# A post-norm transformer layer on one core: Q and K two batches ahead, their parts written once and filled from broadcasts

## The chip, the cores and the metric

One Trainium2 chip; the kernel runs on 1 core. Times are device microseconds (us) of one execution; lower is better. The kernel before has a median of 2144.75 us in 3 runs (2143.95 to 2145.74).

## What is computed

Eight sequences ("batches") of 1024 rows and 256 columns go through one layer, all in float32. Cut to what matters:

```
scores = (Q @ K.T) / sqrt(16) + prior_lambda * mask(|i - j|)     # 16 heads of 16
attn   = softmax(scores);  a = (attn @ V) @ Wo.T + bo
x      = layernorm(x + a)
h      = x @ (tern(w_fc) * s).T + gate * (x @ v.T @ fast_b.T @ u.T)
y      = (relu(h) ** 2) @ (tern(w_proj) * s).T
out    = layernorm(x + y)
```

The weights w_fc and w_proj are rounded to -1, 0, 1 times a scale per row; the mask is a sum of two Gaussian bells around the diagonal.

## The kernel before

**The groups.** The loop of L1508 runs over 512 groups, 64 per batch and 16 for each set of 4 heads (called G below; 32 G in all). One group handles two blocks of 128 keys of a pair of heads: TensorE makes scores e with keys on the partitions (L761, 2 tiles of 128 x 1024; near the diagonal the prior is added by TensorE, L742, or by VectorE, L775), ScalarE takes the exponential (L776), and TensorE weighs V with the exponentials of the group before (L791). The softmax needs the row maxima first: 12 groups ahead (`LEAD`), TensorE makes the same scores with queries on the partitions (s, L665) and VectorE takes the maximum of each row (L677, 2 per group). All e and s tiles come from a ring of three PSUM tiles. Every 8 groups (group 5 of each 8) `set_max` (L688 to L711) turns the maxima into rows: TensorE transposes them (L693), ScalarE and GpSimd split them (L699, L700), SP writes them to DRAM (L702) and four DMAs put them into the stacks of Q (L709).

Twelve groups before the first e (group -12 on), only s and maxima run: the lead-in.

**Stacks.** A stack holds for one head 64 rows of split Q or K (16 dimensions, each as a high and a low part, in the four combinations) and two rows for the maxima. There are two slots of stacks, each for one G: 2 pairs of heads (pr) x 2 heads (a) x K and Q, that is 8 tiles. `fill_stack` (L321, DMA at L315 to L318) reloads a slot at the start of the G before: 8 DMAs of 256 KB, issued by SP, each from 64 rows of 4 KB. The first pair of stacks is read 4 groups later, the second 8 groups later.

**Where the stacks come from.** A Q/K piece (L611) is four matmuls for 128 columns of heads over 256 rows of x; after two pieces ScalarE casts the result to its high part (`two`, L630, one buffer), GpSimd subtracts for the low part (L631), and `write_parts` (L199 to L206) writes it to DRAM: K as two DMAs of 512 KB, Q as one of 512 and two of 256 KB, since the DRAM tile has four planes per row.

**Pieces.** In each group TensorE also does a few pieces of other work from a list of jobs: Q/K pieces (L611), V (L584), transposes of x (L558), the output projection (L991), the feed-forward of the batch before (L1024, 1038, 1065, 1100), and in the first batch the preparation of the ternary weights (L432 to L550; its low-rank part waits for GpSimd at L494). They share one PSUM bank of two halves. A budget per group ("filled") decides how many pieces it takes. Batch b makes the second chunk (128 columns) of Q and K of its own, and the first chunk of those of b + 1.

**Normalizing.** When a chunk of heads is done, deferred steps follow: the sums are read back as `den` (L829), one group later VectorE takes the reciprocal (L834), `back` goes to DRAM (L836), `rec` is read as a broadcast over 16 rows (L841) with the raw output (L844), and GpSimd multiplies (L848). In the last batch one half is done apart (L878 to L887, `rec_third`). The residual's x is loaded (L976) and gets a bias on GpSimd (L982).

**Order.** The program fixes the order of the instructions on every engine as they are written (L1632 on), so SP issues its DMAs, and ScalarE does its work, in the order of the code. DMAs take eight semaphores in turn, and DMA n is issued only when DMA n - 8 has landed.

The lines on which the change turns:

```python
two = p1.tile([P, 2, HALF], F32R, tag="two", name=f"two{name}_{b}_{c}_{half}")   # L629, p1 has bufs=1
nc.scalar.copy(two[:, 0, :], full)                                               # L630
...
queue.dma_start(                                                                 # L316
    stack[name, s, pr, a][at : at + P // 2, cols].bitcast(F32),
    parts_of[name, b, g // 2][src : src + HD, :, cols].rearrange("p l n -> (p l) n"),
)
```

Of the kernel before, what the change touches and what calls it, by code (L numbers as in the profile page):

```python
# [10 lines left out]
F32 = mybir.dt.float32  # L11
# [32 lines left out]
def tile_postln_layer(  # L44
# [44 lines left out]
    dpool = ctx.enter_context(tc.tile_pool(name="dpool", bufs=2, space=bass.MemoryType.DRAM))  # L89
    first = len(nc.cur_bb.bb.instructions)  # L90
# [11 lines left out]
    def load_x(b, half, tag="x"):  # L102
        t = p1.tile([P, QB, D], F32, tag=tag, name=f"x_{b}_{half}")
        nc.sync.dma_start(t, x[b, ts(half, HALF), :].rearrange("(t p) d -> p t d", p=P))
        x_of[b, half] = t

    load_x(0, 0)
# [85 lines left out]
    def new_parts(name, b, c):  # L193
        parts_of[name, b, c] = dpool.tile(
            [P, 4, L], F32, tag=f"parts_{name}", name=f"parts_{name}_{b}_{c}"
        )
        return parts_of[name, b, c]

    def write_parts(name, t, two, half, rows=slice(0, P)):  # L199
        to, two = t[rows, :, ts(half, HALF)], two[rows].bitcast(F32)  # L200
        nc.sync.dma_start(to[:, :2], two)
        if name == "k":
            nc.sync.dma_start(to[:, 2:], two)
        else:
            nc.sync.dma_start(to[:, 2, :], two[:, 1, :])
            nc.sync.dma_start(to[:, 3, :], two[:, 0, :])  # L206
# [106 lines left out]
    def fill_one(name, G, pr, a, queue, cols=slice(0, L)):  # L313
        (b, g), s = divmod(G, NG), G % SLOTS
        at, src = P // 2 * a, HD * ((g % 2) * HG + 2 * pr + a)  # L315
        queue.dma_start(  # L316
            stack[name, s, pr, a][at : at + P // 2, cols].bitcast(F32),
            parts_of[name, b, g // 2][src : src + HD, :, cols].rearrange("p l n -> (p l) n"),  # L318
        )
# [60 lines left out]
    now, jobs = -LEAD, []  # L380
# [50 lines left out]

    def prepare_fc(half):  # L432
# [4 lines left out]
        def first():  # L437
            w = p1.tile([P, n, D], F32, tag="hi", name=f"fc_{half}")
            nc.sync.dma_start(w, w_fc[ts(half, n * P), :].rearrange("(c p) d -> p c d", p=P))
            st["w"] = w  # L440
            st["uT"] = p1.tile([R, HALF], F32, tag="x1T", name=f"uT_{half}")
            pus = [misc(f"pu_{half}_{k}") for k in range(2)]
            for k, pu in enumerate(pus):
                for i in range(2):
                    nc.tensor.matmul(
                        pu[:R, ts(i, P)],
                        u_sb[:, n * half + 2 * k + i, :],
                        ident,
                        start=True,
                        stop=True,  # L450
                    )

            def empty():
                for k, pu in enumerate(pus):
                    nc.scalar.copy(st["uT"][:, ts(k, D)], pu[:R, :])

            return empty
# [9 lines left out]
        def tern(i, pf):  # L467
            w, hc = st["w"][:, i, :], n * half + i
            sc = s_fc[:, hc : hc + 1]
            scales(sc, w, D)  # L470
            ternary(w, sc, f"fc_{half}_{i}")
            full = p1.tile([P, R], F32, tag="lowf", name=f"lowf_{half}_{i}")
            nc.scalar.copy(full, pf)

            def rows():

                inv = p2.tile([P, 1], F32, tag="inv", name=f"inv_{half}_{i}")
                nc.vector.reciprocal(inv, sc)
                nc.gpsimd.tensor_scalar(full, full, inv, gate_c, op0=ALU.mult, op1=ALU.mult)
                low = ones_low[:, 1, :].rearrange("p (a b c r) -> p a b c r", a=2, b=2, c=2)  # L480
                for k in range(2):
                    src = full.unsqueeze(1).to_broadcast([P, 2, R])
                    nc.gpsimd.tensor_copy(low[:, k, 0].bitcast(F32R), src)
                    nc.gpsimd.tensor_sub(low[:, k, 1], src, low[:, k, 0])
                st["rows"] = i

            defer(1, rows)

        def piece(i):
# [20 lines left out]
            (0.5, lambda i=i: piece(i), 2, lambda i=i: st.get("rows") == i) for i in range(n)  # L510
        ]

    def prepare_proj(i):
# [4 lines left out]
        def first():  # L518
            st["w"] = p1.tile([P, FF], F32, tag="hi", name=f"proj_{i}")
            nc.sync.dma_start(st["w"], w_proj[ts(i, P), :])  # L520

        def second():
            st["sc"] = p2.tile([P, 1], F32, tag="sc", name=f"sc_proj_{i}")
            scales(st["sc"], st["w"], FF)
            st["diag"] = p1.tile([P, D], F32, tag="x1T", name=f"diag_{i}")[:, :P]
            nc.gpsimd.tensor_scalar_mul(st["diag"], ident, st["sc"])
            ternary(st["w"][:, :D], st["sc"], f"proj_{i}_0")
# [20 lines left out]
        return [(0.01, first, 0), (0.01, second, 0), (0.3, third, 1)] + [  # L548
# [4 lines left out]
    def transpose_x(b, bank):  # L553
        def piece(half, dc, k):
# [9 lines left out]
            if dc == NDC - 1 and k == 1:  # L564
                x_of.pop((b, half))
                if half == 0:
                    load_x(b, 1)
# [3 lines left out]
            (0.22, lambda half=half, dc=dc, k=k: piece(half, dc, k), 1)  # L571
# [29 lines left out]

    def queries_keys(b, c, bank):
# [4 lines left out]
        def piece(name, half, k):  # L607
# [11 lines left out]
            def empty():  # L619
# [7 lines left out]
                if k == 0:  # L627
                    return
                two = p1.tile([P, 2, HALF], F32R, tag="two", name=f"two{name}_{b}_{c}_{half}")  # L629
# [3 lines left out]
                write_parts(name, t, two, half)  # L633
# [770 lines left out]
    def first_x(b, main):  # L1404

        for f, n in zip(first_chunk[b][0], (-8, -2)):
            main[n] = with_(f, main[n])
        return main

    def jobs_of(b):  # L1410


        qk = queries_keys(b, 1, misc)
        load, early_xv, ahead = [], [], []
        if b + 1 < B:
            load = [(0.0, lambda: load_x(b + 1, 0), 0)]
            xs, vs = transpose_x(b + 1, misc), values(b + 1, misc)
            early_xv, ahead = xs[:4] + vs[: NB // 2], xs[4:]
            ahead = ahead + queries_keys(b + 1, 0, misc) + vs[NB // 2 :]
        if b + 1 < B:  # L1420
            first_chunk[b] = chunk(b, 0, misc)
        if b == 0:
            main = [(0.3, prepare_v, 1)] + [u for i in range(2) for u in prepare_fc(i)]
            main += [u for i in range(D // P) for u in prepare_proj(i)]
            side = ahead[:12] + early_xv[4:] + ahead[12:]
            return load + qk + early_xv[:4], first_x(b, spread(main, side, 0.05, 0.9))
        old = [over[k : k + 2] for k in range(0, len(over), 2)] or [[]] * 4
        if ahead:
            t, q, v = ahead[:4], ahead[4:12], early_xv[4:] + ahead[12:]

            lead = [t[0], t[1], q[0], t[2], q[1], t[3], q[2], q[3], v[4], q[4], q[5]]
            at_end = [[q[6], q[7]], [v[5], v[6]], [v[7]], []]
            main = v[:4] + feed_forward(b - 1, misc, lead, at_end)
            t = early_xv[:4]
        else:

            old_o = old[2] + old[3]
            t, old[2:], lead = [()] * 4, [[], []], [qk[6], qk[7], *old_o]
            main, qk = feed_forward(b - 1, misc, lead), qk[:6]
# [3 lines left out]
        t = [list(u for u in (k,) if u) for k in t]  # L1443
        jobs = load + [qk[0], *old[0], qk[1], *old[1], *qk[2:4]]

        jobs += [*old[2], *t[0], qk[4], *t[1], *old[3], *t[2], qk[5], *t[3], *qk[6:]]
        over[:] = main[-KEPT:] if b + 1 < B else []
        main = main[:-KEPT] if b + 1 < B else main
        return jobs, first_x(b, main) if b + 1 < B else main
# [54 lines left out]
    jobs = [u for part in jobs_of(0) for u in part]  # L1504

    v_first, qk_first, jobs[:7] = values(0, misc), jobs[1:7], jobs[:1]
    early = [u for two in zip(v_first, qk_first) for u in two] + v_first[6:]
    for g in range(-LEAD, total + 1):  # L1508

        now = g  # L1510
        if g == -8:
# [4 lines left out]
        if 0 <= g < total and g % per_batch == 0:  # L1516
            if g:
                assert not jobs
                jobs = [u for part in jobs_of(g // per_batch) for u in part]
# [32 lines left out]
        if g < 0:  # L1552

            n = g + LEAD + 1 - (done >= QSTEP - 1)
            upto = 14 * n // (LEAD - 1)
            if halves == 2:
                work += [early.pop(0)[1] for _ in range(len(early) - 14 + upto)]
        elif g < total:
            left = per_batch - 1 - g % per_batch
            if g == 0:  # L1560
                among = len(jobs)
            if g < per_batch:

                behind = len(jobs) > among * (1 - (g + 1) / (per_batch - 3))
            else:

                spare = left - groups_for(jobs) if g < total - per_batch else 0
            while jobs and halves >= jobs[0][2] and ready(jobs[0]):
                cost = jobs[0][0]
                if g < per_batch:  # L1570
                    if not (cost == 0.0 or behind):
                        break
                    behind = len(jobs) - 1 > among * (1 - (g + 1) / (per_batch - 3))
                elif filled > 0.75 and not (spare < (-1 if near(g) else 2)):
# [3 lines left out]
                cost, piece, room = jobs.pop(larger(jobs) if halves == 1 and g >= per_batch else 0)[:3]  # L1578
# [106 lines left out]
```

## Time and profile before

| what | number |
|---|---|
| median of 3 runs | 2144.75 us |
| the profiled execution | 2146.07 us, of which the span 2144.3 us |
| busy: PE, DVE, ACT, POOL | 97%, 73%, 67%, 43% |
| mean DMA rate over the span | 90 GB/s, 193.55 MB |
| first s matmul, first e matmul | 26.7 us, 61.3 us |
| a batch, first e to first e (third to sixth) | 253.7 to 253.8 us |
| K's fills, Q's fills | 128 of 256 KB; 124 of 256 KB and 8 of 128 KB |

Times in the trace count from the start of the span. The engines are PE (TensorE matmul), PEld (its weight loads), DVE (VectorE), ACT (ScalarE), POOL (GpSimd) and SP (which issues DMAs; SPq is its queue). A line of a wait names who waited, for whom, the total in us, the times and the longest. A line of a timeline gives the start, the length, the engine, the line of the code, the operation and its tiles. A line of a window gives the busy time (and count) of each engine in it, the granted clock of TensorE, the share of the 16 DMA engines that were busy, and GB/s. The landing marks of a DMA (its semaphore's updates, one from each DMA engine that took part) are read from the trace.

### The profile page before, as it was taken

The numbers are of one execution on the slowest core, as the hardware profiler recorded it, in microseconds if no ns is written. First come the engines' busy times: TensorE is split into PE (matmuls) and PEld (weight loads), VectorE is DVE, ScalarE is ACT, GpSimd is POOL, SyncE is SP. The second block draws the span as 40 slices with busy tenths as digits, with TensorE's granted clock in tenths as the row PEclk, the third lists the DMA queues.
The fourth block names the chain that finished last, engine by engine and source line by source line (L and its number), as shares of the span: only waits on it lengthen the run. The fifth ranks groups of instructions, "written<-read, shape, count | busy, mean of one in ns | idle before, by whom it ended". The sixth has DMA issues, their size and how long they took to land.

```text
span 2144.3 us, 38970 instructions
## 1 busy us (share of the span) xinstructions
PE 2073.6 (97%) x14200; PEld 1200.6 (56%) x14200; DVE 1568.2 (73%) x2909; ACT 1440.2 (67%) x2155; POOL 917.2 (43%) x1075
## 2 busy tenths in 40 slices
PE   6999999999999999999999999999999999999997
PEld 3444445555555555556555555555555555555657
DVE  6777777777777777777777777777777777777736
ACT  2566666766777667667777767677676766766754
POOL 5044332344324453345533445335543445455444
PEclk9999999999999999999999999999999999999999
DMA  6423334223433124423233223422343321422010
GB/s 192 124 76 112 77 88 143 68 62 78 124 103 107 56 60 121 137 73 84 72 133 110 76 70 99 132 86 58 78 124 120 90 70 49 138 74 56 23 47 20
DMA packets 110725, 193.55 MB, mean 90 GB/s; under 512 B 21149, under 2 KB 50253, under 8 KB 110533
## 3 DMA queue, kind: packets, MB, share of 16 engines
q1 hardware_dynamic: 109116, 189.48, 31.3%
q8 instruction: 112, 1.84, 0.4%
q10 hardware_dynamic: 1416, 1.58, 0.2%
q14 instruction: 81, 0.66, 0.1%
HBM read 105.19 MB, written 85.69 MB: 89 GB/s over the span
## 4 chain that ended last, share of the span: by engine, by line
PE 80%; DVE 11%; POOL 3%; DMA 3%; issue 2%; ACT 1%; SPq 0%; DVEq 0%; POOLq 0%; ACTq 0%
PE e L761 22%; PE av L791 19%; PE s L665 16%; DVE junk L677 8%; PE misc L1065 5%; PE misc L611 4%; PE misc L1100 4%; PE misc L584 2%; PE misc L991 2%; PE e L742 1%; PE misc L1072 1%; DVE st L949 1%; DMA parts_k<-twok 1%; PE misc L1025 1%; PE misc L558 0%
## 5 line engine op out<-in xcount | busy, mean ns | idle before, releaser
L677 DVE CUSTOM_DVE_ANT_0 junk<-s,wide 128x1024 f32<-128x1024 f32 x1024 | 1249.1, 1220 | 484.1 <-PE s L665 440.5
L776 ACT ACTIVATE exp<-e 128x1024 f32<-128x1024 f32 x1024 | 1027.6, 1024 | 549.2 <-PE e L761 371.3
L761 PE MATMUL e<-st_q,st_k 66*128 66x512 f32 (+1 forms) x2048 | 618.0, 423 | 0.7 <-DMA st_q<-rows 0.4
L791 PE MATMUL av<-exp,v 128*17 128x512 f32 x4096 | 539.8, 598 | 0.0
L761 PEld LDWEIGHTS e<-st_q,st_k 66*128 66x128 f32 (+1 forms) x2048 | 344.0, 189 | 292.8 <-ACT exp L776 95.3
L665 PE MATMUL s<-st_k,st_q 64*128 64x512 f32 x2048 | 393.9, 446 | 40.1 <-DVE pm L677 25.9
L665 PEld LDWEIGHTS s<-st_k,st_q 64*128 64x128 f32 x2048 | 165.3, 185 | 172.3 <-DVE pm L677 88.6
L775 DVE TENSOR_TENSOR e<-e,wide 128x372 f32<-128x372 f32 (+2 forms) x376 | 190.1, 506 | 38.2 <-PE e L761 35.7
L1083 POOL TENSOR_TENSOR rl<-rl 128x512 f32<-128x512 f32 x112 | 116.7, 1042 | 234.1 <-ACT hi L1082 221.1
L791 PEld LDWEIGHTS av<-exp,v 128*17 128x17 f32 x4096 | 68.1, 95 | 185.7 <-issue 184.3
L742 PEld LDWEIGHTS <-ident_q 96*32 96x32 bf16 x2112 | 64.3, 97 | 162.9 <-issue 159.0
L1085 POOL TENSOR_TENSOR lo<-rl,hi 128x512 fp32r<-128x512 f32 x112 | 143.8, 1284 | 8.8
L1120 POOL TENSOR_TENSOR r<-r,sp_row 128x256 f32<-128x256 f32 x56 | 41.1, 734 | 212.0 <-ACT r L1119 212.0
L594 POOL TENSOR_TENSOR v<-v,bv_row 128x256 f32<-128x256 f32 x64 | 44.0, 689 | 191.9 <-ACT v L593 191.9
L1065 PE MATMUL misc<-xhi,wfT 128*128 128x256 f32 x448 | 117.0, 284 | 0.4 <-ACT fullq L626 0.2
L1065 PE MATMUL misc<-xlo,wfT 128*128 128x256 f32 x448 | 115.0, 280 | 0.0
L1100 PE MATMUL misc<-wpT,lo 128*128 128x256 f32 x448 | 112.0, 282 | 2.6 <-POOL lo L1085 2.6
L1100 PE MATMUL misc<-wpT,hi 128*128 128x256 f32 x448 | 114.3, 288 | 0.0
L631 POOL TENSOR_TENSOR twok<-fullk,twok 128x512 fp32r<-128x512 f32 x30 | 38.6, 1287 | 145.3 <-ACT twok L630 143.6
L1078 ACT ACTIVATE rl<-misc,s_fc 128x256 f32<-128x256 f32 x224 | 94.0, 475 | 0.9 <-POOL lo L1085 0.9
L1065 PEld LDWEIGHTS misc<-xhi,wfT 128*128 128x128 f32 x448 | 84.4, 188 | 10.6 <-ACT fullk L626 2.4
L1100 PEld LDWEIGHTS misc<-wpT,lo 128*128 128x128 f32 x448 | 85.3, 190 | 6.7 <-POOL lo L1085 3.2
(233 smaller groups left out, 2351.9 us busy)
## 6 DMA issues: line engine op xcount, KB each, us to landing
st_k<-parts_k SPq DMA_DIRECT2D x128, 256.0 KB
st_q<-parts_q SPq DMA_DIRECT2D x124, 256.0 KB
parts_k<-twok SPq DMA_DIRECT2D x60, 512.0 KB
parts_q<-twoq SPq DMA_DIRECT2D x64, 256.0 KB
parts_q<-twoq SPq DMA_DIRECT2D x30, 512.0 KB
x<-in_L_attn_x_dram SPq DMA_DIRECT2D x16, 512.0 KB
raw_o<-avs SPq DMA_DIRECT2D x248, 32.0 KB
rec<-back SPq DMA_DIRECT2D x30, 256.0 KB
```

What stands on the lines that cost most here:

```text
L611: nc.tensor.matmul(pt, wT[name][:, dc, ts(c, P)], xT[:, dc, ts(2 * half + k, D)], start=(dc == 0), stop=(dc == NDC - 1),)
L665: nc.tensor.matmul(pair[a][:, kh, :], stack["q", s, pr, a][rows, ts(blk, P)], stack["k", s, pr, a][rows, ts(kh, HALF)], start=True, stop=True,
L677: nc.vector.tensor_tensor_reduce(out=junk, in0=t.rearrange("p k n -> p (k n)"), in1=wide[:, LEFT - P * blk : LEFT - P * blk + L], scale=1. ...
L761: nc.tensor.matmul(t[:, a, :], stack["k", s, pr, a][rows, ts(blk, P)], stack["q", s, pr, a][rows, ts(h, HALF)], start=not by_pe, stop=True ...
L775: nc.vector.tensor_add(part, part, add.to_broadcast([P, 2, hi - lo]))
L776: nc.scalar.activation(e, t.rearrange("p a n -> p (a n)"), AF.Exp)
L791: nc.tensor.matmul(av[32 * j : 32 * j + HD + 1, :], v_bufs[b % 2][:, blk, g * HG + j, : HD + 1], es[j // 2][:, ts(j % 2, HALF)], start=(n ...
L1065: nc.tensor.matmul(ph, wfT[:, dc, ts(hc, P)], st[k2][:, dc, :], start=(dc == 0 and k2 == "xhi"), stop=False,)
L1078: nc.scalar.activation(rl[:, ts(k, n)], ph, AF.Relu, scale=s_fc[:, hc : hc + 1])
L1083: nc.gpsimd.tensor_mul(rl, rl, rl)
L1085: sub(lo, rl, hi.bitcast(F32))
L1100: nc.tensor.matmul(py, st[k][:, hc, ts(i, P)], wpT[:, hc, :], start=(hc == 0 and k == "hi"), stop=(hc == NHC - 1 and k == "lo"),)
```

## The change

Six things change together.

1. The parts in DRAM have two planes instead of four (a pool of its own, 6 buffers) and are written by one DMA.
2. That write is not issued at once, but before the next cast into `two`, or two groups later (`unwritten`, `write_pending`).
3. The fills make the copies: K with one DMA whose source repeats the 32 rows (a broadcast in front), Q with two DMAs of 128 KB, each row read twice. A G has 12 fill DMAs instead of 8.
4. Batch b makes Q and K (both chunks) of batch b + 2 and V of b + 1, and x is loaded accordingly earlier; transposes wait until the load was issued two groups before.
5. The weights w_fc and w_proj are loaded a stage ahead (`load_w`): both halves of w_fc at group -2.
6. The first batch takes its pieces from two lists, `prepare` (weights) and `side` (the rest), with limits of their own; the limits in the other batches are changed.

The diff, cut to its core:

```diff
+    dparts = ctx.enter_context(tc.tile_pool(name="dparts", bufs=6, space=bass.MemoryType.DRAM))
...
-            [P, 4, L], F32, tag=f"parts_{name}", name=f"parts_{name}_{b}_{c}"
+            [P, 2, L], F32, tag=f"parts_{name}", name=f"parts_{name}_{b}_{c}"
...
     def write_parts(name, t, two, half, rows=slice(0, P)):
-        to, two = t[rows, :, ts(half, HALF)], two[rows].bitcast(F32)
-        nc.sync.dma_start(to[:, :2], two)
-        if name == "k":
-            nc.sync.dma_start(to[:, 2:], two)
-        else:
-            nc.sync.dma_start(to[:, 2, :], two[:, 1, :])
-            nc.sync.dma_start(to[:, 3, :], two[:, 0, :])
+        nc.sync.dma_start(t[rows, :, ts(half, HALF)], two[rows].bitcast(F32))
...
     def fill_one(name, G, pr, a, queue, cols=slice(0, L)):
...
+        part = parts_of[name, b, g // 2][src : src + HD, :, cols]
+        n, to = part.shape[-1], stack[name, s, pr, a]
+        if name == "k":
+            both = part.rearrange("p l n -> (p l) n").unsqueeze(0).to_broadcast([2, 2 * HD, n])
+            queue.dma_start(to[at : at + P // 2, cols].bitcast(F32), both)
+            return
+        for l in range(2):
+            rows = slice(at + 2 * HD * l, at + 2 * HD * (l + 1))
+            queue.dma_start(
+                to[rows, cols].bitcast(F32), part[:, l : l + 1, :].to_broadcast([HD, 2, n])
+            )
...
+    unwritten = []
+
+    def write_pending():
+        while unwritten:
+            unwritten.pop(0)()
...
+                write_pending()
                 two = p1.tile([P, 2, HALF], F32R, tag="two", name=f"two{name}_{b}_{c}_{half}")
                 nc.scalar.copy(two[:, 0, :], full)
                 nc.gpsimd.tensor_sub(two[:, 1, :], full, two[:, 0, :].bitcast(F32))
                 made[b, c] = made.get((b, c), 0) + 1
-                write_parts(name, t, two, half)
+                unwritten.append(lambda: write_parts(name, t, two, half))
+                defer(2, write_pending)
...
+        if g == -LEAD:
+            load_x(1, 0)
         if g == -8:
             split_prior()
         if g == -2:
             fill_stack(1)
             load_later()
+            load_w(0)
+            load_w(1)
...
-                elif filled > 0.75 and not (spare < (-1 if near(g) else 2)):
+                if filled > 0.75 and not (spare < (-0.5 if near(g) else 2)):
+                    break
+                elif filled > 0.4 and spare > 3:
                     break
```

## Prediction

> **What bounds the kernel now.** I read the page's busy shares and chain first, then the longest waits of TensorE, then the waits of ScalarE and of the DMA queue, then single DMAs in the timeline with the windows beside them.
>
> ```profile
> PE 2073.6 (97%) x14200; PEld 1200.6 (56%) x14200; DVE 1568.2 (73%) x2909; ACT 1440.2 (67%) x2155; POOL 917.2 (43%) x1075
> ...
> PE 80%; DVE 11%; POOL 3%; DMA 3%; issue 2%; ACT 1%; SPq 0%; DVEq 0%; POOLq 0%; ACTq 0%
> ```
>
> TensorE is busy 97% and holds 80% of the chain, so time falls only where TensorE does less or waits less. In the trace a group (from its first e matmul to the next group's) takes 3.58 us with no piece, 3.65 with one Q/K piece and about 4.6 with two pieces: the first piece is nearly free, a second costs 0.75 to 1.
>
> ```profile
> PE s L665 <- DVE pm L677: 25.9, 67, 1.0
> PE s L665 <- DMA st_k<-parts_k: 8.4, 2, 8.1
> ...
> PE misc L494 <- POOL ones_low L484: 4.7, 6, 1.7
> ```
>
> Columns: us in all, times, longest. These are all the waits that the change aims at, some 13 us. ScalarE's wait for the single buffer `two` is small today, because SP issues the parts' write at once:
>
> ```profile
> ACT twoq L630 <- DMA parts_k<-twok: 2.2, 3, 1.3
> ```
>
> A short wait also costs clock. After the 1.67 us wait of L494 the clock was granted at half for 3.4 us:
>
> ```profile
> 195.42:198.83 3.41, 3.41 (x11) 2.49 (x8) 1.79 (x4) 1.80 (x2) 0.00 (x0) 0.50 0.62 192
> ```
>
> Half of 3.41, 1.7 us, is my price for the clock after each long hole.
>
> **Part 1: TensorE's work is moved.** Totals are conserved. Batch 6 loses 16 Q/K pieces; at 0.55 each (between 0.05 alone and 1.0 as second) -8.7. Batch 7 loses 8 and takes over 16 hidden-layer matmuls: -2.3. Batch 0 sheds the L494 waits and the clock after one (4.7 + 1.7, of which I take 5.8) and gets more pieces, mostly single: +1.5. Batches 1 to 5 keep their mix, with more pairs: +1 each, +5. Sum -10.3. At the start one K write instead of two lets fills go 1.5 us sooner (the second landed at 22.87, the fills went at 22.89); that is counted in part 3.
>
> **Part 2: writes are two groups later.** `two` has one buffer, so the next cast (ScalarE, in order) waits until the previous write has landed, and exp stands behind the cast; TensorE then has no e. The order of SP's DMAs in the changed program puts these writes behind others: the write that the last cast before the first exp waits for stands behind 12 fills, 5 loads and two 512 KB weight loads; that of group 13 behind the rows (issued 6.35 into that group, landing 3.2 later, a 512 KB write's time; wanted at 3.7): +5.2; group 57's behind avs: +2. Those of batch 0 group 48, batch 1 group 16, batch 0 group 20 and batches 2 to 5 group 19 stand behind 12 fills. With fills as fast as now (1.2 us for 256 KB) I get 12.5 at the start, 5.5 + 5.1 at the two early ones, 0.5 each at four of the others, and 5 for the clock: with 5.2 and 2, +37. The queue's price before: a wait of 1.34 us made a group 0.7 longer, one of 0.66 nothing, so 0.65 is free.
>
> **Part 3: K's copies come from a broadcast.** This decides. The new K fill reads [2 copies, 32 rows, 1024]; the outermost dimension of its source is 2. Fills now have 64 rows outermost and fill all 16 DMA engines. The nearest row is the last batch's `rec_third`, 256 KB with 4 outermost:
>
> ```profile
> 2038.80 0.58 SPq L882 DMA_DIRECT2D rec_third<-back_third  x1
> 2039.47 0.49 SPq L884 DMA_DIRECT2D o<-raw_o  x1
> 2043.34 0.34 SPq L702 DMA_DIRECT2D rows<-both  x1
> 2049.03 1.13 SPq L709 DMA_DIRECT2D st_q<-rows  x4
> ```
> ```profile
> 2045.00:2046.00 1.00, 1.00 (x9) 0.30 (x2) 0.00 (x0) 0.97 (x2) 0.00 (x0) 1.00 0.25 95
> ```
> ```profile
> SPq L709 <- DMA rows<-both: 96.3, 64, 5.3
> ```
>
> In the window the DMA share is 0.25 at 95 GB/s: 4 engines of 16, 24 GB/s each. Its semaphore got four late marks, 2046.18 to 2046.90, and landed 8.1 us after issue. And it held others up: of the o load behind it 12 marks come by 2044.69 and four at 2047.29 to 2048.84; the 16 KB of rows landed 5.7 us after issue, the 5.3 of the last line, where 64 such waits average 1.5. So each engine works its queue in order, and whatever uses all engines waits for the slowest. DMAs with 8 outermost (rec) leave 8 marks, those with 2 (st_q from rows) leave 2. I take two engines for K.
>
> The Trainium skill, "DMA: Bandwidth & Descriptors", section "Rules for kernel authors", speaks against this edit outright: a leading zero-stride broadcast of c copies confines the DMA to at most c engines. The row for 4 agrees; none here has a large copy on 2. From its 435 GB/s over 16 ports ("Where 436 GB/s comes from") 27 per engine would be an estimate of 4.8 us per copy, and about 2400 for the whole.
>
> By the row: 256 KB over 2 x 24 GB/s is **5.5 us per K copy** (1.2 now). Four per group of heads are 22.1; Q's share on those engines (64 KB each) 2.8; together 24.9 out of a group's 62. With 1.5 until the first packet, the two engines are done at F + 26.4, F being the first fill's issue. Bounds: 1.2 (all 16 engines) and 9.1 (14.4 GB/s per engine, as when all 16 move 230 GB/s during fills now).
>
> Who waits (SP also stops: DMA n waits for DMA n - 8 on its semaphore, so it works off the list at about the copies' pace):
> - Start. K copies one behind the other: first s at 35 instead of 26.7 (fills at 21.4, two copies 11, 2.6 fixed as for rec). The second stacks' fills go at 64.2 (55.86 + 8.3), end at 90.6; two weight loads 4.9; the write 2.6: the first exp at 98 instead of 62.1. **+36.**
> - Batch 0 group 48, batch 1 group 16: cast wanted at F + 8, write landed at F + 29.2 (26.4 less 0.4 for the issue, 3.2 for the write); less 0.65: 20.5 each. **+41.**
> - Batch 0 group 20, batches 2 to 5 group 19: wanted at F + 18.5: 10 each. **+50.**
> - Softmax denominators. The reciprocal on DVE stands between the row maxima; all scores share three PSUM tiles, so DVE's wait stops TensorE within about 1.5 us. In batch 3 it ran 20.2 us after the first fill:
>
> ```profile
> 998.03 0.50 SPq L316 DMA_DIRECT2D st_k<-parts_k  x1
> ...
> 1014.70 0.47 SPq L829 DMA_DIRECT2D den<-sums  x1
> ```
> ```profile
> 1018.34 0.55 DVE L834 RECIPROCAL den<-den 128x64 f32<-128x64 f32 x1
> ```
>
>  Now the sums (behind the fills) land at F + 28, and den, behind one write, at F + 32.5: 12.3 - 1.5 = 11 at group 51 of batches 1 to 6 (in batch 0 the wait above covers it). **+66.** At group 3 of batches 1 to 7 (wanted at F + 19.1) a 512 KB x load stands before it in batches 1 to 5, +2.5: 14 there and 12 in the last two. **+94.**
> - Part 2's two waits without fills: **+7.** Clock after 22 such holes (1 + 1 + 2 + 5 + 13) x 1.7: **+37.**
>
> The first stacks, needed some 17 us after F, have both copies at F + 15, the second (33) at F + 26: no wait, and little to spare. Four more issues per group of heads cost SP 2.4 us, beside waits. Fewer write bytes gain nothing but the start. Weight and x loads a stage ahead are hidden, except in the terms above.
>
> **Sum.** 36 + 41 + 50 + 66 + 94 + 7 + 37 = 331; less 10.3 = +321. The profiled run is 2146.07 (span 2144.3), 1.3 above the median 2144.75: 2146 + 321 - 1.3 = **2465**.
>
> Its own ends: 5.1 us per copy (32 packets of 4 KB per engine at their 159 ns median there) -1.6 per group on 20 waits and -6 at the start: 2425; no clock loss -37; denominators that find 5 us more cover -65: about 2320. Upwards 5.9 (rec_third's marks came 2.94 us after the previous DMA's, 16 packets): 2505; then waits for x at L982 (20.3 us in 15 times now, loads that will queue behind K) and stacks that miss their 2 us: 2600.
>
> **Rivals.**
> 1. *No new wait, faster.* If copies go over all 16 engines, and the writes land before the casts (SP gets round to them because the fills' waits for free stacks come later than I place them), only part 1 and the start count: -10.3 - 1.6 = 2133. For it: ScalarE idles a third, and today's casts wait 2.2 us in all. Against it: the order of the program, and the four-engine row. It decides as long as a write lands within 0.65 us of the cast that wants it.
> 2. *All engines, but queued writes.* +37 - 12 = +25: 2170. Against it, the four-engine row again.
> 3. *Dearer copies.* At 9.1 us each the 20 waits grow by 16 and the start by 26, near 2810, and then the first stacks come late. For it: packets took 304 ns at median over the kernel. Against: two engines do not fill the memory, and beside rec_third they took 159.
>
> **How the numbers follow.** Two engines, 2320 to 2600: 0.76; still dearer, to 2810 and above: 0.12; rival 2: 0.06; rival 1: 0.06. From rival 1 to 2 lies the 0.2% (4.3 us) that a measurement of this kernel can tell from no change; 0.01 of each. Faster 0.05, same 0.02, slower 0.93. The range holds the first case and, to reach 8 in 10, a third of the dear one: 2320 to 2640.
>
> **What would show it.** In the changed profile: K fills landing 8 us or more after issue, stretches with a DMA share of about 0.13 at some 48 GB/s behind each set of fills; `SPq` waits for DMA lanes; ACT twoq L630's equivalent waiting for parts in tens of us; DVE's reciprocal waiting for den; first s near 35; batches of some 290 us instead of 254; half clock after the holes. Fills at 1.2 us each and 230 GB/s would refute part 3; den in time at F + 20 would take 160 us off; and a first exp before 80 would refute the start.

## The result and the profile after

The changed kernel takes 2624.24 us (median of 4 runs, 2622.94 to 2627.67), 1.223 times the kernel before (95% interval 1.221 to 1.225; 2145.24 us in the same comparison). That is 479 us more; the forecast was 2465, some 320 more, with a range of 2320 to 2640. So the time lies in the range, near its upper end, and the rise is half as large again as the forecast's. The profiled execution took 2627.67 us, its span 2625.9; lines of the code have moved by some 29 (L761 is now L790).

The page of the changed kernel, its busy times and its chain:

```profile
PE 2145.8 (82%) x14200; PEld 1237.4 (47%) x14200; DVE 1571.9 (60%) x2909; ACT 1439.5 (55%) x2155; POOL 915.7 (35%) x1075
...
PE 50%; DMA 21%; DVE 9%; POOL 2%; ACT 2%; issue 1%; SPq 1%; DVEq 0%; ACTq 0%; POOLq 0%
DMA st_k<-parts_k 16%; PE e L790 13%; PE av L820 12%; PE s L694 11%; DVE junk L706 6%; PE misc L1129 3%; PE misc L1094 3%; PE misc L638 2%; DMA x<-in_L_attn_x_dram 2%; PE misc L1020 1%; DMA parts_k<-twok 1%; PE misc L605 1%; DMA sums<-avs 1%; PE e L771 1%; PE misc L1101 1%
```

The matmuls are the same in number (14200). TensorE's busy time is 72 us longer, because more of the work runs at half clock: 153 us of its busy time lie where the granted clock was 0.50, against 18 before. Its share falls from 97% to 82%, and DMA, 3% of the chain before, is 21%, of which K's fills alone are 16%. The waits of the changed kernel (in all, times, longest):

```profile
DVE den L863 <- DMA den<-sums: 220.8, 13, 22.6
...
ACT twoq L658 <- DMA parts_k<-twok: 163.7, 11, 28.3
POOL x L1011 <- DMA x<-in_L_attn_x_dram: 163.2, 12, 28.8
```
```profile
PE s L694 <- DMA st_k<-parts_k: 16.5, 2, 12.6
```

None is an engine's wait for a K fill except the last, at the start: what is late is other DMAs, which stand behind K's fills. A window at the start, where only K's first fills are under way:

```profile
27.00:30.00 3.00, 0.00 (x0) 0.00 (x0) 0.00 (x0) 0.00 (x0) 0.00 (x0) 0.50 0.13 48
```

A DMA share of 0.13 is 2 engines of 16, and they move 48 GB/s. In batch 3, K's four fills of the set issued at group 48, at 1272.14, 1274.11, 1276.31 and 1283.76, left their last marks at 1283.09, 1289.34, 1295.29 and 1300.91: one every 5.6 to 6.3 us (over all 32 sets the median is 5.7), where 5.5 and 0.7 for Q's share were forecast. Each K fill leaves three marks: one about 1.0 us after its issue and two late ones, from the two engines; only the last tells that it has landed.

Of the 511 steps from group to group, 29 are longer than 5.5 us (one before). What these have over 3.8 us sums to 448 us. From batch to batch (first e to first e) it takes:

| batch | 0 | 1 | 2 | 3 | 4 | 5 | 6 | 7 (63 steps) |
|---|---|---|---|---|---|---|---|---|
| before | 242.4 | 254.1 | 253.7 | 253.8 | 253.8 | 253.8 | 253.8 | 249.4 |
| after | 320.0 | 325.2 | 315.8 | 317.4 | 318.2 | 320.0 | 280.3 | 282.7 |
| after without what the holes have over 3.8 | 242.0 | 255.1 | 260.0 | 259.6 | 259.4 | 261.0 | 246.7 | 247.5 |

With the first e at 77.6 instead of 61.3, that is the whole difference. (A "hole" is a step from group to group of more than 5.5 us.)

### The profile page after: what moved, and what is told of

It is laid out like the page before. It is cut to its first block, busy times and chain, and to the rows that moved or that the text cites. A ratio compares the mean times of both kernels' runs of the same rounds, so it can differ in the third digit from the quotient of the medians.

```text
span 2625.9 us, 38958 instructions
## 1 busy us (share of the span) xinstructions
PE 2145.8 (82%) x14200; PEld 1237.4 (47%) x14200; DVE 1571.9 (60%) x2909; ACT 1439.5 (55%) x2155; POOL 915.7 (35%) x1075
## 4 chain that ended last, share of the span: by engine, by line
PE 50%; DMA 21%; DVE 9%; POOL 2%; ACT 2%; issue 1%; SPq 1%; DVEq 0%; ACTq 0%; POOLq 0%
DMA st_k<-parts_k 16%; PE e L790 13%; PE av L820 12%; PE s L694 11%; DVE junk L706 6%; PE misc L1129 3%; PE misc L1094 3%; PE misc L638 2%; DMA x<-in_L_attn_x_dram 2%; PE misc L1020 1%; DMA parts_k<-twok 1%; PE misc L605 1%; DMA sums<-avs 1%; PE e L771 1%; PE misc L1101 1%
## 5 line engine op out<-in xcount | busy, mean ns | idle before, releaser
L694 PE MATMUL s<-st_k,st_q 64*128 64x512 f32 x2048 | 419.5, 459 | 428.4 <-DVE pm L706 247.6
L790 PE MATMUL e<-st_q,st_k 66*128 66x512 f32 (+1 forms) x2048 | 632.9, 431 | 4.0 <-DMA st_q<-rows 3.5
L820 PE MATMUL av<-exp,v 128*17 128x512 f32 x4096 | 560.3, 619 | 0.0
L790 PEld LDWEIGHTS e<-st_q,st_k 66*128 66x128 f32 (+1 forms) x2048 | 354.2, 194 | 311.5 <-ACT exp L805 58.7
L694 PEld LDWEIGHTS s<-st_k,st_q 64*128 64x128 f32 x2048 | 180.0, 191 | 560.2 <-DVE pm L706 288.1
L863 DVE RECIPROCAL den<-den 128x64 f32<-128x64 f32 x15 | 8.3, 552 | 220.8 <-DMA den<-sums 220.8
L659 POOL TENSOR_TENSOR twoq<-fullq,twoq 128x512 fp32r<-128x512 f32 x30 | 38.5, 1282 | 275.7 <-ACT twoq L658 275.6
L1094 PE MATMUL misc<-xhi,wfT 128*128 128x256 f32 x448 | 122.7, 296 | 0.8 <-ACT fullq L653 0.2
L658 ACT CAST twoq<-fullq 128x512 fp32r<-128x512 f32 x30 | 18.6, 619 | 164.6 <-DMA parts_k<-twok 163.7
L659 POOL TENSOR_TENSOR twok<-fullk,twok 128x512 fp32r<-128x512 f32 x30 | 38.4, 1280 | 170.1 <-ACT twok L658 170.1
```

The lines of the kernel that those rows point to most:

```text
L694: nc.tensor.matmul(pair[a][:, kh, :], stack["q", s, pr, a][rows, ts(blk, P)], stack["k", s, pr, a][rows, ts(kh, HALF)], start=True, stop=True,
L790: nc.tensor.matmul(t[:, a, :], stack["k", s, pr, a][rows, ts(blk, P)], stack["q", s, pr, a][rows, ts(h, HALF)], start=not by_pe, stop=True ...
L820: nc.tensor.matmul(av[32 * j : 32 * j + HD + 1, :], v_bufs[b % 2][:, blk, g * HG + j, : HD + 1], es[j // 2][:, ts(j % 2, HALF)], start=(n ...
L1094: nc.tensor.matmul(ph, wfT[:, dc, ts(hc, P)], st[k2][:, dc, :], start=(dc == 0 and k2 == "xhi"), stop=False,)
```

## The experiments

Theory E: a K fill runs on two DMA engines since the outermost dimension of its source is 2, and all that follows in the queue waits. Rival Q: the writes' deferral and place in SP's queue do it, whatever the fills. Rival B: reading rows through a broadcast in front is slow in itself.

### K from plain DMAs

```diff
-            both = part.rearrange("p l n -> (p l) n").unsqueeze(0).to_broadcast([2, 2 * HD, n])
-            queue.dma_start(to[at : at + P // 2, cols].bitcast(F32), both)
+            for c in range(2):
+                rows = slice(at + 2 * HD * c, at + 2 * HD * (c + 1))
+                queue.dma_start(to[rows, cols].bitcast(F32), part.rearrange("p l n -> (p l) n"))
```

> The changed kernel, but K's copies come from two plain DMAs of 32 rows each instead of one with a broadcast in front (16 fill DMAs per set of heads instead of 12, bytes and order unchanged). Theory E (the broadcast confines a K fill to two DMA engines, and the queue behind it does the rest): about 2170, holes of 17 to 30 us per group shrink to a few us, no stretch at a DMA share of 0.13. Theory Q (the writes' place in SP's queue and the deferral are the cause, whatever the engines): above 2400. Theory B (reading 32 rows twice is slow in itself, whatever the form): above 2400.

Measured: 2242.18 us, 1.044 times before (1.043 to 1.046). 382 of the 479 us are gone; the longest steps are 17 us, and the reciprocal's wait falls from 220.8 to 29.8. That ends Q as the main cause, and with it that reading the rows twice is slow in itself. 97 us stay, 72 more than the 25 forecast for this case.

### The parts written at once, K's broadcast kept

```diff
-                unwritten.append(lambda: write_parts(name, t, two, half))
-                defer(2, write_pending)
+                write_parts(name, t, two, half)
```

> The changed kernel with the parts written at once after the cast instead of two groups later; K's broadcast stays. Theory E: the casts' waits for the parts' write (some 160 us in the changed kernel) mostly go, the reciprocal's waits (220 us) stay: 2430 to 2500. Theory Q: below 2200.

Measured: 2599.11 us (1.211, 1.209 to 1.213), only 25 less. E is right against Q, but the size is not: the steps at the start, batch 0 groups 14 and 49 and batch 1 group 17 do shrink, while group 19 keeps its 20 us in batches 2 to 5, because the Q/K pieces there come just after the fills are issued: even a write at once stands behind them. In batch 3 that write was issued at 1107.62, behind fills that began at 1089.92, and landed at 1120.11. And new steps appear: 25 and 23 us at group 4 of batch 0 and group 19 of batch 1, where casts wait for the write of Q's parts, and 22 us at group 52 of batch 0, at a den read that the wait at group 49 had covered.

### The broadcast alone, in the kernel before

In these two kernels K's rows stand in another order than Q's, so the scores are others; the work is the same.

```diff
-            [P, 4, L], F32, tag=f"parts_{name}", name=f"parts_{name}_{b}_{c}"
+            [P, 2 if name == "k" else 4, L], F32, tag=f"parts_{name}", name=f"parts_{name}_{b}_{c}"
...
+        part = parts_of[name, b, g // 2][src : src + HD, :, cols].rearrange("p l n -> (p l) n")
+        if name == "k":
+            part = part.unsqueeze(0).to_broadcast([2, 2 * HD, L])
+        queue.dma_start(stack[name, s, pr, a][at : at + P // 2, cols].bitcast(F32), part)
```

> The kernel before, with K's parts in two planes, written once, and K's fill as one DMA with the broadcast in front; nothing else. Theory E: the start 10 us later, the reciprocal waits 10 to 15 us at 14 places and the clock is halved after each: 2300 to 2400. Theory Q: within 5 us of the kernel before, since no write is deferred and no order changed.

Measured: 2451.83 us (1.141, 1.138 to 1.144), 307 more than before and above the range. With nothing deferred and no piece moved, this one DMA costs more than the prediction had for the start, the reciprocals and the clock after these 14 holes together (36 + 66 + 94 + 24 = 220). The kernel's own waits show the same place:

```profile
DVE den L832 <- DMA den<-sums: 179.9, 13, 17.1
```

The other form, two plain DMAs of 32 rows (the loop of the first experiment, in the kernel before):

> The kernel before, with K's parts in two planes, written once, and K's fill as two plain DMAs of 32 rows. Theory E: 2141 to 2145 (the start gains about 1.5, four more issues per set of heads cost nothing). Theory B: as much slower as the kernel with the broadcast in front.

Measured: 2145.43 us, ratio 1.0002 (0.9993 to 1.0012). Writing K once gains nothing that can be measured, not even the 1.5 us at the start, and 4 more issues cost nothing: the loss of 307 us is the broadcast's.

### The number of copies in front

```diff
-            both = part.rearrange("p l n -> (p l) n").unsqueeze(0).to_broadcast([2, 2 * HD, n])
+            both = part.rearrange("p l n -> (p l) n")[: 4 * HD // 4]
+            both = both.unsqueeze(0).to_broadcast([4, 4 * HD // 4, n])
```

> The changed kernel with the same K fill, one DMA of 256 KB with a broadcast in front, but of 4 copies of 16 rows instead of 2 of 32 (so K's rows in the stack are others and the scores differ; bytes, DMAs and order are the same). Theory E (as many engines as copies): a fill takes some 2.8 us on 4 engines, a DMA share of 0.25 behind the fills, and the time lies well between: 2300 to 2390. Theory B (a broadcast in front is slow in itself): about 2624, as with 2.

> The same with a front of 16 copies of 4 rows (K's rows are again others). Theory E: all 16 engines, the time of the kernel with plain K fills, 2230 to 2245. Theory B: about 2624.

Measured: 2406.80 us with 4 (1.121, 1.119 to 1.123), a little above the range, and 2245.20 with 16 (1.046, 1.044 to 1.048), like the plain fills. The reciprocal's waits of the kernels with 4 and with 16 (220.8 with 2):

```profile
DVE den L864 <- DMA den<-sums: 107.4, 13, 13.5
```
```profile
DVE den L864 <- DMA den<-sums: 26.9, 6, 5.3
```

Same bytes, same DMAs, same form: only the size of the outermost dimension differs, and the loss over plain fills is 382, 165 and 3 us. The landing marks say how many engines took part: besides one mark about 1.0 us after the issue, a K fill leaves 2 marks with 2 copies in front and 4 with 4; with 16 it leaves 16 in all. From one K fill's landing to the next it takes 5.7, 3.7 and 2.4 us (medians; 2.4 in the kernel before). With 4 the forecast had 2.8, so its time is above the range. B falls, E is shown.

### What is left with all engines: the queue

Plain K fills and the parts written at once (the edits of the first two experiments together):

> The changed kernel with K's copies as two plain DMAs and the parts written at once. With the engines restored, what is left of the loss (97 us) should lie in the order of the queue: at-once writes take away the start's wait (13), the one of batch 0 group 14 (6) and, as far as the writes then stand before the fills, those of batch 0 group 49 and batch 1 group 17 (7 each), with the clock after each: 2200 to 2215. If the deferral is all of the rest: below 2150.

Measured: 2210.71 us (1.030, 1.029 to 1.032), as expected: 31 less than with plain fills alone, and the four steps named are gone. So the deferral costs about 31 us where fills are fast; part 2 of the prediction had 37.

Then the store of a finished chunk four groups later:

```diff
                 norm_apply(r, r, mv, st["rstd"])
-                nc.sync.dma_start(
-                    out[b, ts(c, CT * P), :].rearrange("(t p) d -> p t d", p=P), r
-                )
+                defer(4, store)
+
+            def store():
+                nc.sync.dma_start(
+                    out[b, ts(c, CT * P), :].rearrange("(t p) d -> p t d", p=P), r
+                )
```

> The same as the run with plain K fills and writes at once, with the DMA that stores a finished chunk of the output put four groups after its computation. Theory: in batches 1 to 5 that store stands ahead of the fills of group 48 and waits some 10 us for GpSimd, which makes the fills late and then the reciprocal (8 us at group 52); moved behind the fills it costs nothing: 35 to 50 us less than the run before it. Rival: the hole of group 52 stays, because the reciprocal waits for something else: no difference.

Measured: 2200.11 us (1.026, 1.024 to 1.027): 11 less, not 35. The step of group 52 went only from 12 to 10.5 us. I had taken one of its causes for the whole. The SP lines of this kernel in batch 3, and GpSimd's:

```profile
1033.38 1.26 SPq L319 DMA_DIRECT2D st_k<-parts_k  x2
...
1041.66 1.18 SPq L323 DMA_DIRECT2D st_q<-parts_q  x2
1042.88 0.58 SPq L1005 DMA_DIRECT2D x<-in_L_attn_x_dram  x1
```
```profile
1047.28 1.44 POOL L1011 TENSOR_TENSOR x<-x,bo_row 128x256 f32<-128x256 f32 x2 [9.80 <-DMA x<-in_L_attn_x_dram]
```

The fills go out in time, but the residual's x load is issued after all of them, and GpSimd waits 9.8 us for it; what VectorE needs from GpSimd comes late, and the row maxima behind it. The same edit in the changed kernel itself:

> The changed kernel with nothing but the output's store put four groups later. Theory: the store that stands ahead of the fills of group 48 holds them up by 10 us in four or five batches, and that is why the reciprocal's wait there is 25 us and not the 11 forecast: 35 to 50 us less than the changed kernel, 2574 to 2590, holes at group 52 of some 15 to 20 us instead of 29. Rival: the copies themselves take longer there: within 10 us of 2624.

Measured: 2579.64 us (1.201, 1.199 to 1.203), 45 less; the steps at group 52 fall from 28.5 to 29.7 to 18.2 to 20.1. There the store was the cause of what the forecast missed.

The order of pieces alone, with the parts and fills of the kernel before:

> The run with plain K fills, writes at once and outputs later (2200), but with the parts in four planes, K written twice, Q in three DMAs, and 8 plain fills of 256 KB, all as in the kernel before: what is left of the change is the order of the pieces and the loads. Theory: half as many fill issues (4.7 us of SP instead of 9.3 per set of heads) bring the x load behind them earlier by 4.6: five holes at group 52 and 4 shrink, 2170 to 2185, and the rest over 2145 is the new order itself (batches 2 to 5 at some 258 without their holes, against 253.8). Rival: the new order is worth its 10 us and only the fills spoil it: 2145 or less.

Measured: 2208.70 us (1.029, 1.028 to 1.031). Neither came true: half as many issues gain nothing, the step of group 52 is still 10.7 to 12.1 us. In batches 2 to 5 the x load is issued 5.7 to 6.4 us after the first fill instead of 9.5 to 10.2, and lands no sooner (13.5 to 15.0 us after it, against 12.9 to 14.1). So it isn't SP's issuing that makes the x load late, but what stands ahead of it in the queue: 2 MB of fills and, in this kernel, twice the write. The last run has that load issued by another engine:

```diff
-            nc.sync.dma_start(x1, x[b, ts(c, n), :].rearrange("(t p) d -> p t d", p=P))
+            nc.scalar.dma_start(x1, x[b, ts(c, n), :].rearrange("(t p) d -> p t d", p=P))
```

> The run with plain K fills, writes at once and outputs later (2200), with the residual's x load issued by ScalarE instead of SP, so that it stands in another queue than the 2 MB of fills. Theory: the hole of group 52 (7 us in batches 2 to 5, and about as much at group 4 of the first two) is the x load waiting behind fills, with GpSimd's bias and then VectorE's statistics behind it; in its own queue the load lands in some 4 us: 15 to 30 us less, 2170 to 2185. Rival 1: the reciprocal (den, still behind the fills) takes the wait over: within 6 us of 2200. Rival 2: ScalarE, in order, waits for the load's buffer and holds exp up: above 2206.

Measured: 2185.06 us (1.019, 1.017 to 1.020), 15 less: GpSimd's wait for x falls from 41.7 to 1.1 us, the step of group 52 is 5.8 to 6.8 us, and den still waits (14.1 before, 16.0 now). But the edit did more than change the queue. In ScalarE's order the load goes out 1.4 us before the first fill and lands 2.7 us after its issue:

```profile
1030.92 0.37 ACTq L1005 DMA_DIRECT2D x<-in_L_attn_x_dram  x1
```
```profile
1032.32 1.02 SPq L319 DMA_DIRECT2D st_k<-parts_k  x2
```

So it is shown that a load ahead of the fills takes the wait away, not that a queue of its own would help a load issued behind them.

Some 41 us above the kernel before are left. In the profiled execution 29 of them are what nine steps of more than 5.5 us have over 3.8 (one such step before), and 13 stand in the groups in between, where batches 2 to 5 take 258.0 to 258.8 us instead of 253.8. The run with the old parts and fills has the same 257.9 to 258.8 there, so these are the new order's, of pieces and loads together. Batch 6 takes 251.2 instead of 253.8.

### The first batch's guard alone

```diff
-                st["rows"] = i
+                st["rows"], st["at"] = i, now
...
-            (0.5, lambda i=i: piece(i), 2, lambda i=i: st.get("rows") == i) for i in range(n)
+            (0.5, lambda i=i: piece(i), 2, lambda i=i: st.get("rows") == i and now > st["at"] + 1) for i in range(n)
```

> The kernel before with one thing of the change: in the first batch, a piece that turns the low-rank rows is taken only two groups after GpSimd was told to make them. Theory: the waits of TensorE for ones_low (4.7 us, and 1.7 for the clock) go, and the pieces pushed back cost up to 2: 2139 to 2142. Rival: what is pushed back pairs up with other pieces and costs as much: 2144 to 2147.

Measured: 2145.06 us against 2147.42 for the kernel before on the same chip, ratio 0.9987 (0.9976 to 0.9997): at most 0.24% less. TensorE's wait at L494 (4.7 us) is gone and the matmuls are as many, but a new step of 7.0 us appears at group 48 of batch 0. This kernel's output differs from the reference's, and why stays open, so this is a time and not a version to keep.

## Why the prediction held, and where its sizes were off

**Right: the cause and its price per copy.** Part 3 took 24 GB/s per engine from one window of `rec_third` and got 48 GB/s for two; the changed kernel shows 48, and a copy every 5.7 us (median; 5.6 to 6.3 in the set above) where 6.2 was worked out with Q's share. So a forecast from four engines held for two. The places were right too: the start, the casts at groups 48 and 16 (49 and 17 as measured here), 20 and 19, and the reciprocals at groups 51 and 3 (52 and 4 here).

**In the range partly by luck.** The prediction's own upper end for two engines was 2600; the last 40 us of its range were added for copies of 9.1 us each, and these did not come: one K copy landed 6.7 us after the one before it at most. The 2624 lies in that addition. The rise was forecast as 321 and is 479; the table shows where the other 160 or so come from.

The terms, as measured by what each step has over 3.8 us (part of the clock's loss is in them, so the forecast's 37 is split by the number of holes; the start also has the later first e):

| term | forecast with clock | measured |
|---|---|---|
| start, until the first exp | 36 + 2 | 44 |
| batch 0 group 48 (49), batch 1 group 16 (17) | 41 + 3 | 49 |
| group 20 of batch 0, 19 of batches 2 to 5 | 50 + 9 | 85 |
| den at group 51 (52 as measured), batches 1 to 6 | 66 + 10 | 128 |
| den at group 3 (4 as measured), batches 1 to 7 | 94 + 12 | 119 |
| batch 0 groups 13 (14) and 57 (56) | 7 + 2 | 9 |
| other steps | 0 | 32 |
| the groups in between | -10 | +16 |

**Off: den at group 51.** F, the issue of a set's first fill, was taken to come at the same place in the groups as in the kernel before. Where it does, the forecast of 12.3 us for this wait was right: 11.9 in batch 1, 10.7 in batch 6. (The rows of the kernel before give 20.3 us from the first fill to the reciprocal, not 20.2, which changes nothing.) In batches 2 to 5 it is 21.4 to 22.6, because in the changed order the store of an output chunk comes before the fills and waits for GpSimd. The SP lines of batch 3, and SP's wait there:

```profile
1271.64 0.40 SPq L1143 DMA_DIRECT2D out_dram<-r  x1
1272.14 0.58 SPq L318 DMA_DIRECT2D st_k<-parts_k  x1
```
```profile
SPq L1143 <- POOL r L989: 10.6, 1, 10.6
```

The fills start at 1272.1, where group 47 begins at 1261.5 and group 48 at 1266.0. The store was part of a moved step, its place was in the order of the program, and the prediction named only the DMAs behind the fills. The run with the store four groups later takes the 10 us back (45 in all).

**Off: group 19.** The casts wait 16 to 17 us, not 10. In batches 2 to 5 the cast was wanted 14.9 us after the first fill where 18.5 was counted, and the write landed 31.0 to 32.0 after it where 29.2 was counted. In batch 3 (the first fill, the write, the cast):

```profile
1114.89 0.55 SPq L318 DMA_DIRECT2D st_k<-parts_k  x1
...
1143.91 0.56 SPq L203 DMA_DIRECT2D parts_k<-twok  x1
```
```profile
1147.01 0.62 ACT L658 CAST twoq<-fullq 128x512 fp32r<-128x512 f32 x1 [17.17 <-DMA parts_k<-twok]
```

**Off: the first copy of a set.** From issue to landing it takes 10.8 us (median of the 32 sets, 9.9 to 12.3), where 1.5 until the first packet and 5.5 to 6.2 for the copy were counted. So the last K copy lands 28.4 us after F (median), not 26.4. Why is not settled. A store ahead of it can hardly be the reason in batch 3 (it had landed at 1273.79); but from 1278 to 1280, with two engines busy, only 37 GB/s were moved:

```profile
1278.00:1280.00 2.00, 2.00 (x13) 1.55 (x9) 1.76 (x4) 1.09 (x3) 0.00 (x0) 1.00 0.13 37
```

**Off: the start.** The first s came at 30.61, not 35, when one K copy had landed (30.41) and the second had not (35.21); but the second stacks' fills went at 71.15, not 64.2, and the first exp at 107.0, not 98.

**Off: the clock.** It was priced at half of 3.41 us for each of 22 holes, 37 in all. After the hole at group 52 of batch 3 TensorE worked at half clock for more than 5 us, and over the run its work takes 72 us longer; how much of that is in the span was not measured.

**Off: part 1.** The forecast had -10.3 for the moved work; the groups between the holes give +16.5. Batches 6 and 7 gain 7.1 and 1.9 (8.7 and 2.3 forecast), but batches 2 to 5 lose 5.6 to 7.2 each, not 1. With most of the holes gone (the run with x issued by ScalarE) these batches still have 258.0 to 258.8 besides them, so 4 to 5 each are the order's: about 19 us, more than batches 6 and 7 give. The other 1 to 2 may be the clock after the holes. Which pieces do it was not tried.

**Not seen:** x loads behind the fills that stop GpSimd or TensorE (batch 1 group 38, batch 7 group 21, and part of the wait at group 4, where TensorE's transpose waited 17.6 us for x). The prediction had them as a reason for the upper end only.

The rivals: copies on all engines with queued writes was forecast at 2170; the run that makes this case takes 2242, since the x load behind the fills, the store and the order of pieces were missing in it too. The case of no new wait at all was not reached by any run with the new order.

Not tried: a second buffer for `two`.

## What to carry to other kernels

Before replacing copies by a broadcast source, look at the outermost dimension of the access pattern: a broadcast of 2 or 4 copies in front put a large DMA on 2 or 4 engines here, and the cost shows up at whatever comes next in the queue, more than at the DMA itself. In a kernel that TensorE bounds at 97%, bytes saved on a queue with slack are worth nothing (2145.4 against 2144.8 with K written once), while an order of issue that puts a needed load or a waiting store around a large fill costs at once. When a change moves steps, write down every DMA that the new order puts ahead of the large ones as well as behind them.

## What the runs showed of the hardware that was not expected

Each DMA on fewer than 16 engines that was read here leaves one mark more than it has engines: K's fills leave three on 2 engines and five on 4, `rec` nine on 8 (the prediction counted the late ones alone). The first comes about 1.0 us after the issue; on two engines that is some 9 to 11 us before the first copy of a set has landed. The loss grows 2.3 times from 4 engines to 2: with 2, 4 and 16 copies in front of the same 256 KB it was 382, 165 and 3 us over plain fills.

TensorE's granted clock falls during the wait, not only after it: in batch 3 TensorE stops at about 1285 and goes on at 1308.6; the clock is 1.00 until 1290 and half from then until 1313.9.

```profile
1286.00:1288.00 2.00, 0.00 (x0) 0.00 (x0) 0.00 (x0) 0.00 (x0) 0.00 (x0) 1.00 0.23 78
...
1290.00:1292.00 2.00, 0.00 (x0) 0.00 (x0) 0.00 (x0) 0.00 (x0) 0.00 (x0) 0.50 0.55 165
...
1309.00:1313.00 4.00, 4.00 (x15) 1.47 (x15) 2.57 (x5) 2.39 (x5) 1.59 (x2) 0.50 0.56 163
1313.00:1314.00 1.00, 1.00 (x5) 0.61 (x5) 0.00 (x0) 1.00 (x2) 0.72 (x1) 0.56 0.00 0
```
